# Two-layer vision Mamba on one core: scan outputs by pairs of blocks, a later LayerNorm product, and one turning copy per half unit

## The chip, the cores and the metric

The kernel runs on one core of one Trainium2 chip. Its time is the device time of one launch, in microseconds (us). Three runs of the kernel before took 16030.84, 16043.01 and 16072.04 us; their median, 16043.01 us, is the time before. The profile is one more execution, described below.

## The reference, cut to what matters

Eight images of 64 x 64 positions with 192 channels go through two layers, all in fp32. Layer 0 is a Mamba-2 block with an MLP behind it. Layer 1, the one that the change is in, works on halves of 96 channels:

```
fused = concat(conv_branch(x[..., :96]), ss2d(x[..., 96:])) + x
xr_n = LN(xr) * ln_g + ln_b                   # over 96 channels
xi, z = split(xr_n @ in_proj)                 # 192 + 192
u = silu(depthwise3x3(xi))                    # and u with rows and columns exchanged
y = selective scan of u in four directions    # state 16, 192 channels, 4096 steps
y = y0 + flip(y2) + turned back(y1 + flip(y3)) + D * u
out = (LN(y) * out_norm_g + out_norm_b) * silu(z) @ out_proj    # LN over 192, out 96
```

## The kernel before

**The main loop** is `selective_scan`. It cuts the scan of layer 1 into 3072 units, 384 per image: eight (direction pair, quarter) steps of three channel tiles of 16 units. A unit is 128 rows (8 channels x 16 states) by 1024 positions. For each unit q the loop sends out, engine by engine: a load of the decay input, 512 KB, six units ahead (`fetch`, L1435, on SP's queue); Exp on ScalarE (`decay`, L1440), in pairs, two and three units ahead, after every odd unit; two matmuls that spread the input over the states (`spread`, L1448), one unit ahead, into one of two PSUM buffers; the product with B on VectorE (`weigh`, L1465); the scan on VectorE (`scan`, L1472), the product with C on GpSimd (L1475); and for every four units a sum over states on TensorE with a ScalarE copy (`gather`, L1486 and L1491). `prepare` makes the next tile's inputs, and its transfers `dud` and `dus` are on SP's queue too. Every engine works through its instructions in the order in which they are sent out, and so does SP with the transfers.

**The other work** is written as generators that yield a cost for TensorE work, or None. `Beside` deals it out: each unit has two half units, and in each one `half` (L1280) adds the rate to a credit and runs the current generator until the credit is spent, or until a None, which ends the half unit whatever the credit. A yield of None is therefore a delay: what comes after it is sent out at least one half unit later. Unspent credit is carried, up to one rate. `spread_over` sets the rate when an image begins: 450 / halves + work / (halves - 9 x generators), where `work` is the sum of the known costs. While image i is scanned, these generators run in turn for images i+1 and i-1: `conv0`, `ssd`, `mlp0` (layer 0 of i+1), `conv_branch` and `scan_outputs` (of i-1, with `scan_sums` beside the branch), `scan_inputs` and `transposed` (of i+1). Image 0's scan has no i-1, image 7's has only two `conv_branch` and one `scan_outputs`; layer 0 and the scan inputs of image 0 run ahead of the loop; `scan_sums` and `scan_outputs` of image 7 run behind it, in the tail.

At unit 360 of an image's 384, `Beside.finish` (L1296) runs whatever is left of the generators at once, without regard to yields, since at units 360 to 362 the next image's scan input is loaded (`load`, L1349), and from unit 363 on TensorE projects it (`project`, L1362). At unit 362 the next `conv0` begins.

**`scan_outputs`** (L1193) takes the 4096 positions in eight blocks of 512. Its 192 channels are a tile of 128 rows and one of 64. Per block: load of both; mean by two matmuls (L985), subtraction on VectorE (L989), squares on ScalarE (L992); variance by two matmuls (L1001), Ln and Exp in PSUM on ScalarE (L1003, L1004), product on VectorE (L1008); scale and shift on ScalarE (L1230), two matmuls for z and two Silu (L1234, L1236); product on GpSimd (L1243); projection by two matmuls (L1248, L1249), addition on VectorE (L1253), store. `center` and `normalize`, which hold L985 to L1008, also serve `scan_inputs`, there for 96 channels. PSUM tiles for all of this come from `cx.one` (L88), a ring of four buffers in the loop, shared with `gather`, `project` and `prepare`.

**`transposed`** (L1094) makes u with rows and columns exchanged: four loads of the first 128 channels, each followed by a None (the last by two), then eight copies of 1024 columns on ScalarE (L1114), four for 128 channels and four for 64, through four buffers `part`; each copy is stored by SP (L1122).

Of the kernel before, what the change touches and what calls it, by code (L numbers as in the profile page):

```python
# [105 lines left out]
def setup(cx, cp, dp, tp, p0, p1):  # L106
# [3 lines left out]
    def const(src, shape, tag):  # L110
        t = cp.tile(shape, F32, tag=tag, name=tag)
        nc.sync.dma_start(out=t, in_=src)
        return t

    ident = k["ident"] = cp.tile([128, 128], F32, tag="ident", name="ident")
    make_identity(nc, ident)

# [63 lines left out]
    k["conv3_b"] = const(p1["conv3_b"].unsqueeze(1), [CH, 1], "conv3_b")  # L181
    k["in_proj"] = const(p1["in_proj"], [128, 2 * DI], "in_proj")
    k["out_a"] = const(p1["out_proj"][0:128], [128, CH], "out_a")
    k["out_b"] = const(p1["out_proj"][128:DI], [DI - 128, CH], "out_b")
    k["xp"] = const(p1["xp"].rearrange("g t p m -> p g t m"), [128, 2, 3, NXP], "xp")

    k["dtw"] = cp.tile([NXP, 2, 3, 128], F32, tag="dtw", name="dtw")
# [17 lines left out]
    for n, rows in (("a", slice(0, 128)), ("b", slice(128, DI))):  # L205
        size = rows.stop - rows.start
        for v in ("out_norm_g", "out_norm_b"):
            k[v + n] = const(p1[v][rows].unsqueeze(1), [size, 1], v + n)
    k["dwb"] = cp.tile([128, 3], F32, tag="dwb", name="dwb")
    for i in range(2):  # L210
        nc.sync.dma_start(out=k["dwb"][64 * i : 64 * (i + 1)], in_=p1["dw_b"].rearrange("(j p) -> p j", p=64))
# [22 lines left out]
    for n, c0, c1 in (("xa", 0, 128), ("xb", 128, DI), ("za", DI, DI + 128), ("zb", DI + 128, 2 * DI)):  # L234
        ps = cx.one("ps_b")
        nc.tensor.matmul(ps[: c1 - c0, 0:1], lhsT=k["in_proj"][:CH, c0:c1], rhs=ln_b, start=True, stop=True)
        k["bias_" + n] = cp.tile([128, 1], F32, tag="bias_" + n, name="bias_" + n)
        nc.vector.tensor_copy(k["bias_" + n][: c1 - c0], ps[: c1 - c0, 0:1])
    nc.vector.tensor_scalar_mul(k["in_proj"][:CH], k["in_proj"][:CH], ln_g)
    for n, size in (("m96", CH), ("m192", DI)):  # L240
        k[n] = cp.tile([128, 128], F32, tag=n, name=n)
# [59 lines left out]
def in_turn(items, *stages):  # L301

    for turn in range(len(items) + len(stages) - 1):
        for lag in reversed(range(len(stages))):
            if 0 <= turn - lag < len(items):
                yield from stages[lag](items[turn - lag])
# [669 lines left out]
def center(cx, xs, sizes, means, squares):  # L976

    nc, pin = cx.nc, cx.pin
    n = max(sizes)
    ps = cx.one("ps_mean")
    for i, (x, m) in enumerate(zip(xs, means)):
        pin(nc.tensor.matmul(ps[:n], lhsT=m, rhs=x, start=i == 0, stop=i == len(xs) - 1))  # L985
    yield 1.2 * len(xs)
    yield None
    for x, size in zip(xs, sizes):
        pin(nc.vector.tensor_sub(x[:size], x[:size], ps[:size]))  # L989
    yield None  # L990
    for x, size, s in zip(xs, sizes, squares):
        pin(nc.scalar.activation(s[:size], x[:size], AF.Square))  # L992


def normalize(cx, xs, sizes, means, squares):

    nc, pin = cx.nc, cx.pin
    n = max(sizes)
    ps = cx.one("ps_var")
    for i, (x, m) in enumerate(zip(squares, means)):  # L1000
        pin(nc.tensor.matmul(ps[:n], lhsT=m, rhs=x, start=i == 0, stop=i == len(xs) - 1))  # L1001

    pin(nc.scalar.activation(ps[:n], ps[:n], AF.Ln, bias=cx.k["eps"][:n]))  # L1003
    pin(nc.scalar.activation(ps[:n], ps[:n], AF.Exp, scale=-0.5))  # L1004
    yield 1.2 * len(xs)
    yield None
    for x, size in zip(xs, sizes):
        pin(nc.vector.tensor_mul(x[:size], x[:size], ps[:size]))  # L1008

# [84 lines left out]
def transposed(cx, u):  # L1094

    nc, pin = cx.nc, cx.pin
    with cx.pool("t1") as tp:
        wholes = []
        for n, src in enumerate((u[0], u[2][0:64])):
            wholes.append(tp.tile([src.shape[0], L], F32, tag=f"whole{n}", name=f"whole{n}"))  # L1100

        def load(n, q):
            here = slice(q * L // 4, (q + 1) * L // 4)
            pin(nc.sync.dma_start(out=wholes[n][:, here], in_=(u[0], u[2][0:64])[n][:, here]))

        for q in range(4):
            load(0, q)
            yield from pause(1 if q < 3 else 2)
        front = []
        for whole, dst in zip(wholes, (u[1], u[2][64:128])):  # L1110
            for q in range(4):
                w0 = q * WW // 4
                part = tp.tile([whole.shape[0], L // 4], F32, tag="part", name="part", bufs=4)
                pin(nc.scalar.copy(part.rearrange("p (w h) -> p w h", h=HH), wh(whole)[:, w0 : w0 + WW // 4, :]))  # L1114
                front.append((dst[:, q * L // 4 : (q + 1) * L // 4], part))
                if whole is wholes[0]:
                    load(1, q)
                if q % 2 == 1:
                    yield 1.0
                    yield None  # L1120
                if len(front) == 2:
                    pin(nc.sync.dma_start(out=front[0][0], in_=front.pop(0)[1]))  # L1122
        pin(nc.sync.dma_start(out=front[0][0], in_=front.pop(0)[1]))
# [69 lines left out]
def scan_outputs(cx, y, xn, short, out):  # L1193

    nc, pin, k = cx.nc, cx.pin, cx.k
    parts = (("a", 0, 128), ("b", 128, DI))
    with cx.pool("e1", 2) as ep:
        st = {}
        sizes = (128, DI - 128)
        xns = [ep.tile([128, 512], F32, tag=f"xn{i}", name=f"xn{i}", bufs=1) for i in range(3)]  # L1200
        for v in xns:
            pin(nc.gpsimd.memset(v[CH:], 0.0))

        def cols(r):
            return slice(r * 512, (r + 1) * 512)

        means = [k["m192"], k["m192"][: DI - 128]]

        def load(r):
            st[r] = {}  # L1210
            for n, src in (("a", y[0]), ("b", y[2][0:64])):
                v = st[r][n] = ep.tile([src.shape[0], 512], F32, tag="v" + n, name="v" + n, bufs=7)
                pin(nc.sync.dma_start(out=v, in_=src[:, cols(r)]))
            if r == 0:
                yield from pause(4)
            yield 0.0

        def mean(r):
            pin(nc.sync.dma_start(out=xns[r % 3][:CH], in_=xn[:, cols(r)]))
            sq = st[r]["sq"] = [ep.tile([n, 512], F32, tag=f"sq{n}", name=f"sq{n}") for n in sizes]  # L1220
            yield from center(cx, [st[r]["a"], st[r]["b"]], sizes, means, sq)

        def norm(r):
            yield from normalize(cx, [st[r]["a"], st[r]["b"]], sizes, means, st[r].pop("sq"))

        def gate(r):
            x = xns[r % 3]
            for n in "ab":
                v = st[r][n]
                pin(nc.scalar.activation(v, v, AF.Identity, scale=k["out_norm_g" + n], bias=k["out_norm_b" + n]))  # L1230
            for n, c0, c1 in parts:
                size = c1 - c0
                ps = cx.one("ps_z")[:size]
                pin(nc.tensor.matmul(ps, lhsT=k["in_proj"][:, DI + c0 : DI + c1], rhs=x, start=True, stop=True))  # L1234
                z = st[r]["z" + n] = ep.tile([size, 512], F32, tag="z" + n, name="z" + n)
                pin(nc.scalar.activation(z, ps, AF.Silu, bias=k["bias_z" + n][:size]))  # L1236
                yield 1.2
            sh = st[r]["sh"] = ep.tile([CH, 512], F32, tag="sh", name="sh", bufs=3)
            pin(nc.sync.dma_start(out=sh, in_=short[:, cols(r)]))

        def apply(r):
            for n in "ab":
                pin(nc.gpsimd.tensor_mul(st[r][n], st[r][n], st[r].pop("z" + n)))  # L1243
            yield 0.0

        def project(r):
            ps = cx.one("ps_o")[:CH]
            pin(nc.tensor.matmul(ps, lhsT=k["out_a"], rhs=st[r]["a"], start=True, stop=False))  # L1248
            pin(nc.tensor.matmul(ps, lhsT=k["out_b"], rhs=st[r]["b"], start=False, stop=True))  # L1249
            yield 2.4  # L1250
            yield None
            o = st[r]["o"] = ep.tile([CH, 512], F32, tag="o", name="o")
            pin(nc.vector.tensor_add(o, ps, st[r]["sh"]))  # L1253

        def store(r):
            pin(nc.sync.dma_start(out=out[:, cols(r)], in_=st.pop(r)["o"]))
            yield 0.0

        def ahead(r):
            yield 0.0  # L1260

        yield from in_turn(range(NB), load, ahead, mean, norm, gate, apply, project, store)


class Beside:
# [304 lines left out]
def vision_mamba_pair_kernel(ctx: ExitStack, tc: tile.TileContext, x: bass.AP, p0: dict, p1: dict, out: bass.AP):  # L1570
# [44 lines left out]
    with tc.tile_pool(name="ps_a", bufs=4, space=PSUM) as more:  # L1615
        cx.singles.append(more)
        stages(0)
        beside.finish()
        beside.costs.update(conv_branch=190.0, scan_outputs=78.0)
        cx.singles.remove(more)  # L1620

    def tail():
# [104 lines left out]
```

## Time and profile before

The profiled execution took 16027.31 us, of which its span, first instruction to last, is 16025.4 us. All the times below are microseconds from the span's start.

| stretch | what runs | us |
|---|---|---|
| 0 to 893.9 | ahead of the loop: layer 0 and scan inputs of image 0 | 893.9 |
| 893.9 to 2681.3 | units of image 0 | 1787.4 |
| 2681.3 to 14263.7 | units of images 1 to 6 | 1905.2 to 1941.3 each |
| 14263.7 to 15787.3 | units of image 7 | 1523.6 |
| 15787.3 to 16025.4 | tail | 238.1 |

A group of instructions is shown as line, engine, operation, tiles, shapes, count, then busy us, mean ns of one, and the engine's idle time before them with what ended it. A window is shown as its length and each engine's busy us, the share of full speed that TensorE's clock was granted (PEclk), the share of DMA time in use, and GB/s. A wait is shown as the engine and line that waited, what it waited for, us in total, times, and the longest.

### The profile page before, as it was taken

To read this page: it belongs to the slowest core of one execution; us is meant where nothing else is said; L and a number is where in the kernel's file an instruction comes from. 1 tells how busy PE (TensorE), PEld (TensorE's weight loads), DVE (VectorE), ACT (ScalarE), POOL (GpSimd) and SP (SyncE) were. 2 spreads that over 40 slices of the span, in tenths; PEclk is the share of its full clock that TensorE was granted. 3 is DMA by queue.
4 is the path that set the end of the run, shared out by engine and by line. 5 is a ranking of instruction groups with operands and counts; after the bars stand their busy time and mean duration, and the time that the engine had idled before them with its cause. 6 is when DMAs were issued, how large, how long until landed. Compare 5 with 4: busy or idle time off the path is not lost. (4 is left out here: it accounts for less than half of the span.)

```text
span 16025.4 us, 207140 instructions
## 1 busy us (share of the span) xinstructions
PE 12969.3 (81%) x69608; PEld 4558.8 (28%) x69608; DVE 12232.0 (76%) x9262; ACT 9059.2 (57%) x13776; POOL 10981.2 (69%) x8165
## 2 busy tenths in 40 slices
PE   8977888789887898778878788787888778877766
PEld 4423322333223322233213332233322333211111
DVE  2268887887778877788678886788867887778994
ACT  3355566555665557655466565664656555655653
POOL 3258776876668766687667876678766776667783
PEclk9987888789887898878978799887988879879887
DMA  3288888878787887978878788887888878888885
GB/s 89 86 213 197 212 206 222 198 206 225 199 227 186 214 221 194 226 187 220 218 199 212 191 221 220 209 213 193 220 208 214 205 197 232 202 228 218 212 217 136
DMA packets 1604247, 3243.11 MB, mean 202 GB/s; under 512 B 389424, under 2 KB 843056, under 8 KB 1603184
## 3 DMA queue, kind: packets, MB, share of 16 engines
q1 hardware_dynamic: 1603184, 3229.84, 79.5%
q8 instruction: 556, 9.11, 0.3%
q14 instruction: 507, 4.15, 0.1%
HBM read 2550.93 MB, written 678.18 MB: 201 GB/s over the span
## 5 line engine op out<-in xcount | busy, mean ns | idle before, releaser
L1475 POOL TENSOR_TENSOR h<-h,bc 128x1024 f32<-128x1024 f32 x3072 | 7239.2, 2357 | 1334.9 <-DVE h L1472 1039.1
L1472 DVE TENSOR_TENSOR_SCAN h<-dA,carry,dB 128x1024 f32<-128x1024 f32 x3072 | 7200.3, 2344 | 479.5 <-ACT dA L1440 152.3
L1465 DVE TENSOR_TENSOR dB<-dB,bc 128x1024 f32<-128x1024 f32 x3072 | 3736.6, 1216 | 1665.2 <-PE dB L1448 1625.0
L1440 ACT ACTIVATE dA<-dA,neg_a 128x1024 f32<-128x1024 f32 x3072 | 3373.9, 1150 | 84.9 <-DMA dA<-dld 78.6
L1486 PE MATMUL acc<-h,gather 128*32 128x512 f32 x12288 | 2169.0, 703 | 319.0 <-POOL h L1475 134.7
L1474 POOL COPY carry<-h 128x1 f32<-128x1 f32 x2304 | 421.6, 183 | 2482.3 <-DVE h L1472 2344.5
L1448 PE MATMUL dB<-dus,spread 48*128 48x512 bf16 x6144 | 1401.2, 433 | 886.1 <-DVE h L1472 842.8
L1491 ACT COPY y<-acc 128x512 f32<-128x512 f32 x1536 | 890.2, 580 | 1842.1 <-issue 1014.9
L884 PE MATMUL ps_c<-p,conv_w 128*96 128x512 f32 x2304 | 1165.5, 628 | 37.3 <-ACT p L904 37.3
L1448 PEld LDWEIGHTS <-spread 48*128 48x128 bf16 x6144 | 321.2, 95 | 2969.5 <-issue 1374.7
L687 PE MATMUL ps_y<-X,M 64*64 64x64 f32 x12288 | 622.2, 277 | 433.3 <-issue 200.1
L336 PE MATMUL ps_cv<-pad,diag 64*64 64x512 f32 x6912 | 852.6, 606 | 19.6 <-ACT y L1491 13.0
L615 ACT ACTIVATE M<-ps_d,ln_dt 128x64 f32<-128x64 f32 x3072 | 666.5, 337 | 275.5 <-PE ps_d L621 206.8
L687 PEld LDWEIGHTS ps_y<-X,M 64*64 64x64 f32 x12288 | 567.7, 186 | 602.2 <-issue 256.5
L1486 PEld LDWEIGHTS acc<-h,gather 128*32 128x32 f32 x12288 | 290.7, 115 | 1223.3 <-issue 522.6
L609 ACT COPY bc<-ps_t 64x256 f32<-64x256 f32 x256 | 93.5, 365 | 917.1 <-PE ps_t L604 917.0
L620 PE MATMUL ps_d<-R,after 128*128 128x384 f32 x1024 | 572.7, 650 | 35.5 <-ACT bc L609 16.1
L1440 ACT ACT_TABLE_LOAD x445 | 570.9, 1283 | 7.9
L884 PEld LDWEIGHTS ps_c<-p,conv_w 128*96 128x96 f32 x2304 | 346.2, 167 | 721.9 <-issue 645.2
L1362 PE MATMUL ps_xp<-u,xp 128*128 128x512 f32 x768 | 471.1, 700 | 92.7 <-DMA u<-u 78.5
L1400 POOL TENSOR_TENSOR du<-dl,u 128x1024 f32<-128x1024 f32 x192 | 452.2, 2355 | 96.2 <-DMA bcd<-rows 81.0
L366 PE MATMUL ps_h<-oa,w1a 128*128 128x256 f32 x1536 | 456.0, 417 | 64.0 <-ACT y L1491 23.3
(248 smaller groups left out, 17979.2 us busy)
## 6 DMA issues: line engine op xcount, KB each, us to landing
dA<-dld SPq DMA_DIRECT2D x3072, 512.0 KB
dud<-terms SPq DMA_DIRECT2D x192, 768.0 KB
dus<-dud SPq DMA_DIRECT2D x1152, 128.0 KB
bc<-bcd SPq DMA_DIRECT2D x256, 512.0 KB
y<-yrows SPq DMA_DIRECT2D x256, 384.0 KB
u<-u SPq DMA_DIRECT2D x192, 512.0 KB
dld<-dl SPq DMA_DIRECT2D x192, 512.0 KB
y<-y SPq DMA_DIRECT2D x3072, 32.0 KB
```

The costliest lines, as they stand in the source:

```text
L336: pin(nc.tensor.matmul(ps[64 * b : 64 * (b + 1)].rearrange("p (h w) -> p h w", w=WW), lhsT=diag[:, t, :], rhs=pad[64 * i : 64 * (i + 1), b ...
L615: pin(nc.scalar.activation(M[:, d, h, :], ps[:, h * S : (h + 1) * S], AF.Exp, bias=bias))
L620: pin(nc.tensor.matmul(ps, lhsT=k["after"], rhs=flat(R[:, d * NH : (d + 1) * NH, :]), start=True, stop=False))
L687: pin(nc.tensor.matmul(psy[d][here, h * HP : (h + 1) * HP], lhsT=M[here, d, h, :], rhs=X[here, d, h, :], start=True, stop=True,))
L884: pin(nc.tensor.matmul(ps.rearrange("p (h w) -> p h w", w=WW), lhsT=w[:, t, :], rhs=pad[:, dy : dy + RB, dx : dx + WW], start=t == 0, stop ...
L1440: pin(nc.scalar.activation(dAs[q], dAs[q], AF.Exp, scale=k["neg_a"][:, steps[m][1], t, i : i + 1]))
L1448: pin(nc.tensor.matmul(dBs[q][:, half, :], lhsT=k["spread"][here, i % 2, :], rhs=du_of[n][here, i // 2, :], start=True, stop=True,))
L1465: pin(nc.vector.tensor_mul(dBs[q], dBs[q], of(q)[0]))
L1472: pin(nc.vector.tensor_tensor_scan(order(h, g), order(dA, g), order(dB, g), carry, ALU.mult, ALU.add))
L1475: pin(nc.gpsimd.tensor_mul(h, h, C_))
L1486: pin(nc.tensor.matmul(ps[32 * v : 32 * (v + 1)], lhsT=k["gather"], rhs=hs[q - 3 + v][:, here], start=True, stop=True))
L1491: pin(nc.scalar.copy(y[:, here], ps))
```

## The change

- `scan_outputs` takes four pairs of blocks. The 128 channels of a pair lie beside each other in a tile of 128 x 1024, the 64 channels of both blocks below each other in one of 128 x 512. The helper `both` sends out the two full matmuls and then two 64-row matmuls on different halves of the array. Constants for the 64 channels are held twice (three more small loads in `setup`, and a copy of `bias_zb` on SP's queue).
- The variance product is sent out a half unit later: one more `yield None` in `normalize`, and two ahead of the product in the new `norm`.
- `transposed` yields after each copy, where it did after every second.
- The planner's known cost of `scan_outputs` goes from 78 to 60.

```diff
@@ normalize
     yield 1.2 * len(xs)
     yield None
+    yield None
     for x, size in zip(xs, sizes):
         pin(nc.vector.tensor_mul(x[:size], x[:size], ps[:size]))
@@ transposed
-                if q % 2 == 1:
-                    yield 1.0
-                    yield None
+                yield 1.0
+                yield None
@@ scan_outputs
+        def both(pss, wa, xa, wb, xb):
+            for ps, x in zip(pss, xa):
+                pin(nc.tensor.matmul(ps, lhsT=wa, rhs=x, start=True, stop=False))
+                yield 1.2
+            for ps, low in zip(pss, lows):
+                pin(nc.tensor.matmul(ps, lhsT=wb[low], rhs=xb[low], start=False, stop=True))
+        def parts(p, pss):
+            a, b = st[p]["a"], st[p]["b"]
+            for j, low in enumerate(lows):
+                yield a[:, j, :], pss[j]
+                yield b[low], pss[j][low]
+        def mean(p):
+            pss = [cx.one("ps_mean") for j in range(2)]
+            a, b = st[p]["a"], st[p]["b"]
+            yield from both(pss, k["m192"], [a[:, j, :] for j in range(2)], k["m192"], b)
+            yield 1.2
+            yield None
+            for i, (v, ps) in enumerate(parts(p, pss)):
+                pin(nc.vector.tensor_sub(v, v, ps))
+                if i == 1:
+                    yield None
+            yield None
+            sqs = [ep.tile([128, n, 512], F32, tag=f"sq{n}", name=f"sq{n}", bufs=1) for n in (2, 1)]
+            pin(nc.scalar.activation(wide(sqs[0]), wide(a), AF.Square))
+            pin(nc.scalar.activation(sqs[1][:, 0, :], b, AF.Square))
+            st[p]["sq"] = sqs
+            yield None
+        def norm(p):
+            pss = [cx.one("ps_var") for j in range(2)]
+            sa, sb = st[p].pop("sq")
+            yield from both(pss, k["m192"], [sa[:, j, :] for j in range(2)], k["m192"], sb[:, 0, :])
+            for ps in pss:
+                pin(nc.scalar.activation(ps, ps, AF.Ln, bias=k["eps"]))
+            for ps in pss:
+                pin(nc.scalar.activation(ps, ps, AF.Exp, scale=-0.5))
+            pin(nc.sync.dma_start(out=wide(xns[p % 2])[:CH], in_=xn[:, cols(p)]))
+            yield 1.2
+            yield None
+            yield None
+            for v, ps in parts(p, pss):
+                pin(nc.vector.tensor_mul(v, v, ps))
+            yield None
+        def gate(p):
+            x = xns[p % 2]
+            for n in "ab":
+                v = wide(st[p]["a"]) if n == "a" else st[p]["b"]
+                pin(nc.scalar.activation(v, v, AF.Identity, scale=k["out_norm_g" + n], bias=k["out_norm_b" + n]))
...
+            for j in range(2):
+                ps = cx.one("ps_z")
+                pin(nc.tensor.matmul(ps, lhsT=k["in_proj"][:, DI : DI + 128], rhs=x[:, j, :], start=True, stop=True))
+                pin(nc.scalar.activation(za[:, j, :], ps, AF.Silu, bias=k["bias_za"]))
+                yield 1.2
+            ps = cx.one("ps_z")
+            for j, low in enumerate(lows):
+                pin(nc.tensor.matmul(ps[low], lhsT=k["in_proj"][:, DI + 128 :], rhs=x[:, j, :], start=True, stop=True))
+            pin(nc.scalar.activation(zb, ps, AF.Silu, bias=k["bias_zb"]))
+            yield 1.2
...
-        yield from in_turn(range(NB), load, ahead, mean, norm, gate, apply, project, store)
+        yield from in_turn(range(NP), load, ahead, mean, norm, gate, apply, project, store)
@@ vision_mamba_pair_kernel
-        beside.costs.update(conv_branch=190.0, scan_outputs=78.0)
+        beside.costs.update(conv_branch=190.0, scan_outputs=60.0)
```

More of the change, by code (lines that the diff above doesn't have):

```diff
@@ L113, in const, with twofold @@
         return t
+    def twofold(src, width, tag):
+        t = cp.tile([128, width], F32, tag=tag, name=tag)
+        for i in range(2):
+            nc.sync.dma_start(out=t[64 * i : 64 * (i + 1)], in_=src)
+        return t
     ident = k["ident"] = cp.tile([128, 128], F32, tag="ident", name="ident")
@@ L183, in setup @@
     k["out_a"] = const(p1["out_proj"][0:128], [128, CH], "out_a")
-    k["out_b"] = const(p1["out_proj"][128:DI], [DI - 128, CH], "out_b")
+    k["out_b"] = twofold(p1["out_proj"][128:DI], CH, "out_b")
     k["xp"] = const(p1["xp"].rearrange("g t p m -> p g t m"), [128, 2, 3, NXP], "xp")
@@ L207, in setup @@
         for v in ("out_norm_g", "out_norm_b"):
-            k[v + n] = const(p1[v][rows].unsqueeze(1), [size, 1], v + n)
+            src = p1[v][rows].unsqueeze(1)
+            k[v + n] = const(src, [size, 1], v + n) if n == "a" else twofold(src, 1, v + n)
     k["dwb"] = cp.tile([128, 3], F32, tag="dwb", name="dwb")
@@ L238, in setup @@
         nc.vector.tensor_copy(k["bias_" + n][: c1 - c0], ps[: c1 - c0, 0:1])
+        if n == "zb":
+            nc.sync.dma_start(out=k["bias_zb"][64:128], in_=k["bias_zb"][0:64])
     nc.vector.tensor_scalar_mul(k["in_proj"][:CH], k["in_proj"][:CH], ln_g)
@@ L1195, in scan_outputs, with cols, wide, load @@
     nc, pin, k = cx.nc, cx.pin, cx.k
-    parts = (("a", 0, 128), ("b", 128, DI))
+    NP = NB // 2
+    lows = [slice(64 * j, 64 * (j + 1)) for j in range(2)]
     with cx.pool("e1", 2) as ep:
         st = {}
-        sizes = (128, DI - 128)
-        xns = [ep.tile([128, 512], F32, tag=f"xn{i}", name=f"xn{i}", bufs=1) for i in range(3)]
+        xns = [ep.tile([128, 2, 512], F32, tag=f"xn{i}", name=f"xn{i}", bufs=1) for i in range(2)]
         for v in xns:
             pin(nc.gpsimd.memset(v[CH:], 0.0))
[L1204 to L1214, printed above, removed]
+        def cols(p):
+            return slice(p * 1024, (p + 1) * 1024)
+        def wide(t):
+            return t.rearrange("p j l -> p (j l)")
+        def both(pss, wa, xa, wb, xb):
[4 more added lines that the diff above has]
+                pin(nc.tensor.matmul(ps, lhsT=wb[low], rhs=xb[low], start=False, stop=True))
+        def load(p):
+            a = ep.tile([128, 2, 512], F32, tag="va", name="va", bufs=4)
+            pin(nc.sync.dma_start(out=wide(a), in_=y[0][:, cols(p)]))
+            b = ep.tile([128, 512], F32, tag="vb", name="vb", bufs=4)
+            for j, low in enumerate(lows):
+                pin(nc.sync.dma_start(out=b[low], in_=y[2][0:64, (2 * p + j) * 512 : (2 * p + j + 1) * 512]))
+            st[p] = {"a": a, "b": b}
+            if p == 0:
@@ L1215, in load @@
                 yield from pause(4)
             yield 0.0
[L1218 to L1227, printed above, removed]
+        def parts(p, pss):
[3 more added lines that the diff above has]
+                yield b[low], pss[j][low]
@@ L1228, in gate @@
+        def gate(p):
+            x = xns[p % 2]
             for n in "ab":
-                v = st[r][n]
+                v = wide(st[p]["a"]) if n == "a" else st[p]["b"]
                 pin(nc.scalar.activation(v, v, AF.Identity, scale=k["out_norm_g" + n], bias=k["out_norm_b" + n]))
[L1231 to L1236, printed above, removed]
-                yield 1.2
@@ L1238, in gate @@
-            sh = st[r]["sh"] = ep.tile([CH, 512], F32, tag="sh", name="sh", bufs=3)
-            pin(nc.sync.dma_start(out=sh, in_=short[:, cols(r)]))
-        def apply(r):
-            for n in "ab":
-                pin(nc.gpsimd.tensor_mul(st[r][n], st[r][n], st[r].pop("z" + n)))
-            yield 0.0
[L1246 to L1253, printed above, removed]
@@ L1255, in store @@
-        def store(r):
-            pin(nc.sync.dma_start(out=out[:, cols(r)], in_=st.pop(r)["o"]))
+            za = st[p]["za"] = ep.tile([128, 2, 512], F32, tag="za", name="za")
+            zb = st[p]["zb"] = ep.tile([128, 512], F32, tag="zb", name="zb")
+            for j in range(2):
+                ps = cx.one("ps_z")
+                pin(nc.tensor.matmul(ps, lhsT=k["in_proj"][:, DI : DI + 128], rhs=x[:, j, :], start=True, stop=True))
+                pin(nc.scalar.activation(za[:, j, :], ps, AF.Silu, bias=k["bias_za"]))
+                yield 1.2
@@ new lines, in gate, with apply @@
+            ps = cx.one("ps_z")
+            for j, low in enumerate(lows):
+                pin(nc.tensor.matmul(ps[low], lhsT=k["in_proj"][:, DI + 128 :], rhs=x[:, j, :], start=True, stop=True))
+            pin(nc.scalar.activation(zb, ps, AF.Silu, bias=k["bias_zb"]))
+            yield 1.2
+            sh = st[p]["sh"] = ep.tile([CH, 2, 512], F32, tag="sh", name="sh")
+            pin(nc.sync.dma_start(out=wide(sh), in_=short[:, cols(p)]))
+        def apply(p):
+            for n in "ab":
+                pin(nc.gpsimd.tensor_mul(st[p][n], st[p][n], st[p].pop("z" + n)))
+                yield 0.0
+            if p == NP - 1:
+                yield from pause(4)
@@ new lines, in project, with store @@
+        def project(p):
+            pss = [cx.one("ps_o")[:CH] for j in range(2)]
+            a, b = st[p]["a"], st[p]["b"]
+            yield from both(pss, k["out_a"], [a[:, j, :] for j in range(2)], k["out_b"], b)
+            yield 1.2
+            yield None
+            o = st[p]["o"] = ep.tile([CH, 2, 512], F32, tag="o", name="o", bufs=1)
+            for j, ps in enumerate(pss):
+                pin(nc.vector.tensor_add(o[:, j, :], ps, st[p]["sh"][:, j, :]))
+        def store(p):
+            pin(nc.sync.dma_start(out=out[:, cols(p)], in_=wide(st.pop(p)["o"])))
+            yield 0.0
@@ L1257, in store, with ahead @@
+        def ahead(p):
             yield 0.0
-        def ahead(r):
-            yield 0.0
-        yield from in_turn(range(NB), load, ahead, mean, norm, gate, apply, project, store)
+        yield from in_turn(range(NP), load, ahead, mean, norm, gate, apply, project, store)
 class Beside:
```

## The prediction

> **What bounds the kernel now.** I read the page's busy shares and groups first, then windows around each generator of one image, then VectorE's waits in those windows, then the timeline of ScalarE where the copies run.
>
> ```profile
> PE 12969.3 (81%) x69608; PEld 4558.8 (28%) x69608; DVE 12232.0 (76%) x9262; ACT 9059.2 (57%) x13776; POOL 10981.2 (69%) x8165
> ...
> L1472 DVE TENSOR_TENSOR_SCAN h<-dA,carry,dB 128x1024 f32<-128x1024 f32 x3072 | 7200.3, 2344 | 479.5 <-ACT dA L1440 152.3
> L1465 DVE TENSOR_TENSOR dB<-dB,bc 128x1024 f32<-128x1024 f32 x3072 | 3736.6, 1216 | 1665.2 <-PE dB L1448 1625.0
> ```
>
> No engine is full. VectorE is the loop's pacemaker: a unit alone costs it 2.34 + 1.22 us, and with a 0.13 us gap the last units start every 3.60 us. 3072 units at 3.60 are 11,060 of the loop's 14,893 us; the rest is VectorE's own side work, which the change leaves as it is (ten products and sums of about 0.67 us per pair of blocks, before and after), and its waits. So I count **VectorE's waits**. Windows in image 3 (conv_branch, scan_outputs, scan_inputs, transposed):
>
> ```profile
> core 0: us, PE busy (x) PEld busy (x) DVE busy (x) ACT busy (x) POOL busy (x), PEclk, DMA share, GB/s
> 7695.00:7990.00 295.00, 274.02 (x772) 74.85 (x771) 193.27 (x110) 121.22 (x153) 180.02 (x148) 0.97 0.88 225
> 7990.00:8138.00 148.00, 119.53 (x287) 27.94 (x290) 112.51 (x92) 119.55 (x142) 100.66 (x79) 0.77 0.72 179
> 8138.00:8338.00 200.00, 175.29 (x768) 42.65 (x762) 152.43 (x99) 136.29 (x161) 121.12 (x90) 0.82 0.77 197
> 8338.00:8379.00 41.00, 10.26 (x47) 1.70 (x46) 25.42 (x15) 29.73 (x26) 23.16 (x11) 0.63 0.87 249
> ```
>
> conv_branch is TensorE's. scan_outputs has three engines near 80%, none full: waits in a circle. VectorE's waits in scan_outputs, then in scan_inputs:
>
> ```profile
> DVE va L1008 <- ACT ps_var L1004: 17.0, 7, 4.8
> DVE va L989 <- DMA y<-y: 4.2, 1, 4.2
> DVE dB L1465 <- PE dB L1448: 3.9, 2, 2.6
> DVE o L1253 <- PE ps_o L1249: 3.1, 2, 2.4
> ```
>
> ```profile
> DVE xt L1008 <- ACT ps_var L1004: 19.6, 7, 4.5
> DVE dB L1465 <- PE dB L1448: 19.6, 9, 4.2
> DVE xt L989 <- PE ps_mean L985: 4.2, 1, 4.2
> ```
>
> In both the LayerNorm product's wait for Ln and Exp is among the largest. The copies of `transposed`, on ScalarE:
>
> ```profile
> 8343.18 0.56 ACT L1491 COPY y<-acc 128x512 f32<-128x512 f32 x1
> 8351.04 7.50 ACT L1114 COPY part<-whole 128x1024 f32<-128x1024 f32 x4 [7.30 <-issue]
> 8362.47 3.73 ACT L1114 COPY part<-whole 64x1024 f32<-64x1024 f32 x2 [3.93 <-DMA whole<-u]
> 8366.10 1.04 ACT L1408 CAST terms<-du 128x1024 bf16<-128x1024 f32 x1
> 8367.05 2.18 ACT L1440 ACTIVATE dA<-dA,neg_a 128x1024 f32<-128x1024 f32 x2
> ```
>
> Six copies and their loads hold the queue for 23 us, and the next decay stands behind them: VectorE waits 14.7 us for dA there, once per image.
>
> **The change part by part.** Against the profiled execution's own 16027.3 us:
>
> *The planner's count.* The costs are constants, so the half units follow by stepping the credit. An image's rate falls from 450/768 + 1140.8/705 = 2.204 to 450/768 + 1126.8/705 = 2.184. Half units per generator, images 1 to 6: conv0 147 to 148, ssd 183 to 187, mlp0 178 to 180, conv_branch 109 to 111, scan_outputs 51 to 49, scan_inputs 81 to 85. `transposed` had nine and six were free behind it; now four are left. Its loads go out, then the flush at unit 360 sends **all eight copies in a row**: in images 1 to 6 "one copy per half unit" does not happen. Only image 0's gets its 13.
>
> *scan_outputs, six images.* ScalarE per pair, before: squares 4 x 0.63, Ln 2 x 0.66, Exp 2 x 0.58, scale 4 x 0.80, Silu 4 x 0.68, six table loads of 1.28: 18.6 us. After: three loads, three Silu, Ln and Exp as they were; Square and Identity of 128 x 1024 from SBUF are not in the trace, so I bound them by the 1.15 of L1440 (same shape) and by twice 0.63 or 0.80; with 1.15 and 1.4 it is 12.3 us. 25 us per image leave an engine at 81%. TensorE: sixteen matmuls per pair become twelve slots, if 64-row pairs run together; L368 on the two halves shows four passes in 1.98 us, so they do. But the four-buffer ring now has two buffers for mean, two for variance, three for z: the second variance matmul takes z's first buffer and waits for its Silu, behind scale (2.2), a load (1.28) and Silu (0.69). The next `spread` is queued behind that matmul, and VectorE waits for it. From the order of instructions, ScalarE reaches that Silu 8.7 us after the subtractions, VectorE needs `spread` after 5.9 to 7.1, and matmul and `spread` take 2: 3 to 5 us in two pairs of four. With the first load 4, the first variance 4 to 5, the drain 3 and some 4 more I get 23 where 33 were (34 in the view, with trifles). **-10 x 6 = -60**; bounds 0 (all comes back through the ring) and -18 each, -108.
>
> The ScalarE saving, by row and rule: a 1.28 us load is followed by its Ln 1.30 us after its start, and twelve fewer per image are 15 us, already within the 25. The Trainium skill, "ScalarE: Activation LUTs", section "What ACT_TABLE_LOAD costs", puts a drain of 1.38 us on top, 2.66 in all; by that the twelve would be 32 us. This trace shows no such drain, so the row stands.
>
> *scan_outputs in image 7*, at a lower rate: **-7** (+5 to -15).
>
> *scan_inputs, seven images.* Of 19 us of waiting for Ln and Exp per image (133 in seven), a half unit more, 1.8 us at least, covers most: one wait is 2.7 on average. TensorE then catches up less: it was busy 175 of 200 us and its own wait behind VectorE was 8. At 90% it needs some 185 for the old work in two more units, where VectorE's least is 164; before, 195 plus two bare units, 202. That is -17; I take -12, as the convolution goes out in bigger bursts (up to 16 matmuls in a half unit, before 14). **-84** (0 to -126).
>
> *The other generators* get 3.5 units more for the same matmuls, in stretches that wait for TensorE: **-2 x 6 = -12** (0 to -24). The shifted order has 60 more table loads elsewhere in the program (55 of them for dA): 77 us of ScalarE at 57%, mostly beside other work: **+14** (0 to +56).
>
> *transposed.* Image 0's copies spread out: 21 us of waiting to 16, **-5** (0 to -12). In the six others, eight copies in place of six stand before a decay, 3.8 us more; the cover is a half unit longer. SP is held too: each store waits for its copy, and behind the stores queue u's loads, six-ahead dA loads, `dud`, `dus` and conv0's first loads. u's last load waits for the last store; the projection at unit 363 waits on TensorE, with `spread` behind it: some 5 us. dA's loads are six units ahead and survive. **+6 x 6 = +36** (0 to +220, as the second rival prices it).
>
> *Tail.* Before, a block is one circle of 11.0 us: 9 of ScalarE, then 1.94 waiting for two products and a subtraction. A pair: 11.7 of ScalarE and 4 of VectorE, 15.7 for 22.0. Three circles save 19; filling and draining by pairs costs some 9 (two more matmuls, one at half clock being 2 us; a 2.36 GpSimd product for 1.26). **-10** (+8 to -20). *Setup:* four more issues at 0.5, **+2** (0 to +5).
>
> The clock, in this trace: passes of 128 x 512 start 0.43 us apart, or 0.85 after an idle stretch; PEclk is 0.97 in conv_branch, 0.77 in scan_outputs. With less for TensorE there the share can fall further; my -10 has no TensorE time in it. The Trainium skill, "TensorE: Matmul & The Clock Gate", section "HAM oscillation", has the array at half clock after idle stretches beyond about 3.4 us; by that rule a quarter fewer slots could be given back whole, which speaks against the pairs. The sum does not need them.
>
> **Sum:** -60 - 7 - 84 - 12 + 14 - 5 + 36 - 10 + 2 = **-126 us**. The profiled execution is 16 us below the median of the runs; I apply the sum to the median: 16043 - 126 = **15,917**.
>
> **The rivals.**
> 1. *The waits return on TensorE.* What VectorE no longer waits for Exp, it waits for `spread`, in both stages. For: dB's wait is already 1625 us, and TensorE is at 88% in scan_inputs. Against: TensorE itself waits for VectorE's scan behind each product. Outputs and inputs give nothing: -126 + 151 = +25, **16,068**.
> 2. *The flush decides: slower.* From the first load of `whole` (8339.8) to unit 368 (8428.4) a chain of loads, copies, stores, u's loads, projection and conv0 takes 89 us, covered by 15 units; now it begins 5.5 units later. If it does not shrink, 20 us per image are laid bare; with two more copies (4), u's last load behind the last store (6) and cold matmuls after it (7) it is 37 x 6 = 222 in place of 36: +60, **16,103**. It decides from (162 + 48) / 6 = 35 us per image. For: DMA at 0.87 in that window, with 249 GB/s. Against: u's loads were not late for lack of data but because SP came to them at unit 360.
> 3. *The circle in scan_outputs opens* and the flush costs nothing: 8 more per image in outputs, 5 in inputs, 6 in the flush: -126 - 48 - 35 - 36 = -245, **15,798**.
>
> That the copies don't spread as the change says is counted already.
>
> **Chances.** Forecast 0.52, rival 1 0.18, rival 2 0.13, rival 3 0.17. A measurement of this kernel can tell about 0.3%, 48 us, from no change: faster 0.70 (forecast, rival 3, less the forecast's weak end), same 0.17, slower 0.13. All bounds together reach 15,738 to 16,337; they don't fall together. Leaving out rival 2's half and rival 3's far side: **15,795 to 16,060**.
>
> **What would show it.** Right: L1008 waiting under 5 us per image in scan_inputs; scan_outputs 49 half units with table loads 14 where 26 were; eight copies in a row, VectorE waiting 13 to 20 us for dA at unit 363, and 5 more for `spread`. Wrong: dB's wait grown by more than L1008's fell (rival 1); over 35 us more between units 357 and 368 (rival 2); ring waits of 5 us in every pair; a tail longer than 238 us.

## The result and the profile after

The changed kernel takes **16,099.56 us** (median of 8 runs, 16,079.48 to 16,117.92) where the kernel before, run beside it, took 16,032.67 (8 runs, 16,017.76 to 16,072.04): ratio 1.0043, 95% interval 1.0033 to 1.0053. It is some 67 us slower. The forecast was 126 us faster, and the time lies above the range.

The profiled execution took 16,085.16 us, its span is 16,083.4. On the page, the busy times and the two VectorE groups of the scan:

```profile
PE 12801.7 (80%) x69608; PEld 4565.5 (28%) x69608; DVE 12229.3 (76%) x9262; ACT 8933.2 (56%) x13578; POOL 10942.1 (68%) x8093
...
L1532 DVE TENSOR_TENSOR_SCAN h<-dA,carry,dB 128x1024 f32<-128x1024 f32 x3072 | 7201.2, 2344 | 547.2 <-ACT dA L1500 229.7
L1525 DVE TENSOR_TENSOR dB<-dB,bc 128x1024 f32<-128x1024 f32 x3072 | 3734.6, 1216 | 1738.0 <-PE dB L1508 1730.1
```

No engine has more to do: TensorE, ScalarE and GpSimd are busy for less time than before and VectorE for as long. The added time is all in waits, and two of VectorE's have grown: for dA (152 to 230 us) and for the product that spreads the input (1625 to 1730).

Windows of image 3 (window's length, busy us of each engine, clock, DMA share, GB/s): mlp0, conv_branch, scan_outputs, scan_inputs, and the stretch from scan_inputs' end to the first transfers of the next conv0:

```profile
core 0: us, PE busy (x) PEld busy (x) DVE busy (x) ACT busy (x) POOL busy (x), PEclk, DMA share, GB/s
7329.00:7751.00 422.00, 354.48 (x1684) 153.71 (x1680) 344.69 (x245) 265.75 (x348) 286.54 (x168) 0.92 0.84 215
7751.00:8057.00 306.00, 279.25 (x777) 77.45 (x778) 195.38 (x112) 128.11 (x160) 181.56 (x149) 0.93 0.86 216
8057.00:8202.00 145.00, 93.24 (x286) 24.88 (x284) 111.72 (x90) 91.20 (x106) 92.83 (x68) 0.78 0.78 197
8202.00:8389.00 187.00, 166.52 (x776) 40.87 (x776) 157.37 (x102) 140.94 (x167) 128.99 (x91) 0.88 0.80 203
8389.00:8437.00 48.00, 11.69 (x30) 2.09 (x30) 23.28 (x13) 26.93 (x21) 18.95 (x10) 0.54 0.82 228
```

The two stages that the change rewrites are shorter: scan_outputs 145 us where 148 were, scan_inputs 187 where 200 were. The first row is the surprise. mlp0, in which not a line was changed, stood like this in the kernel before:

```profile
7290.00:7695.00 405.00, 355.28 (x1681) 153.11 (x1684) 342.07 (x242) 254.63 (x339) 282.23 (x166) 0.93 0.85 222
```

The same TensorE work within 1 us, nearly the same clock (0.93 and 0.92), VectorE's work within 3 us, and 17 us longer. VectorE's largest wait in that window, before and after:

```profile
DVE dB L1465 <- PE dB L1448: 47.9, 34, 10.1
```

```profile
DVE dB L1525 <- PE dB L1508: 62.9, 26, 5.9
```

Fewer waits, and together 15 us more. Counted stage by stage over the whole loop (VectorE's gaps of more than 0.1 us between the units at which the planner starts and ends a generator, summed over all images; "around the copies" is transposed, the free units behind it, and units 360 to 362, with image 7's last units), with the four kernels of the first two groups of experiments that change one thing each:

| VectorE idle, us | before | rate alone (b_rate) | flush alone (b_flush) | later product alone (b_late) | pairs alone (b_pairs) | changed kernel | changed kernel, old rate (a_rate) |
|---|---|---|---|---|---|---|---|
| conv0 | 350 | 363 | 447 | 374 | 330 | 499 | 378 |
| ssd | 668 | 678 | 678 | 677 | 680 | 686 | 690 |
| mlp0 | 431 | 535 | 431 | 444 | 431 | 524 | 433 |
| conv_branch | 720 | 740 | 723 | 729 | 728 | 742 | 721 |
| scan_outputs | 253 | 320 | 243 | 248 | 206 | 221 | 212 |
| scan_inputs | 307 | 272 | 306 | 279 | 296 | 199 | 298 |
| around the copies | 143 | 150 | 69 | 174 | 179 | 75 | 155 |

The changed kernel against before: mlp0 +93, conv0 and the copies together +81, conv_branch and ssd +40, scan_inputs -108, scan_outputs -32. Outside the loop the setup costs 4 us more and the tail 17 less (221.1 us).

### The profile page after: what moved, and what is told of

The parts are those of the page before. It is cut to its first block, busy times and chain, and to the rows that moved or that the text cites. A ratio compares the mean times of both kernels' runs of the same rounds, so it can differ in the third digit from the quotient of the medians.

```text
span 16083.4 us, 206660 instructions
## 1 busy us (share of the span) xinstructions
PE 12801.7 (80%) x69608; PEld 4565.5 (28%) x69608; DVE 12229.3 (76%) x9262; ACT 8933.2 (56%) x13578; POOL 10942.1 (68%) x8093
## 5 line engine op out<-in xcount | busy, mean ns | idle before, releaser
L1546 PE MATMUL acc<-h,gather 128*32 128x512 f32 x12288 | 2115.1, 694 | 406.5 <-POOL h L1535 113.3
L1508 PE MATMUL dB<-dus,spread 48*128 48x512 bf16 x6144 | 1332.2, 428 | 774.8 <-DVE h L1532 720.3
```

The lines of the kernel that those rows point to most:

```text
L1508: pin(nc.tensor.matmul(dBs[q][:, half, :], lhsT=k["spread"][here, i % 2, :], rhs=du_of[n][here, i // 2, :], start=True, stop=True,))
L1546: pin(nc.tensor.matmul(ps[32 * v : 32 * (v + 1)], lhsT=k["gather"], rhs=hs[q - 3 + v][:, here], start=True, stop=True))
```

## The experiments

**First question: the parts, or the planner's rate?** My theory on seeing mlp0: the change lowers the planner's known cost of scan_outputs from 78 to 60 (and raises that of transposed from 4 to 8), so the rate falls from 2.204 to 2.184, and this alone deals mlp0's work out worse and leaves no half units for the copies. The rival: the new code itself costs the time.

```diff
a_rate, the changed kernel:
-        beside.costs.update(conv_branch=190.0, scan_outputs=60.0)
+        beside.costs.update(conv_branch=190.0, scan_outputs=74.0)
b_rate, the kernel before:
-        beside.costs.update(conv_branch=190.0, scan_outputs=78.0)
+        beside.costs.update(conv_branch=190.0, scan_outputs=64.0)
b_late, the kernel before (late=True from scan_inputs only):
     yield 1.2 * len(xs)
     yield None
+    if late:
+        yield None
b_pairs: the changed kernel's scan_outputs and setup; normalize and transposed of before; cost 78
```

> The changed kernel, with the planner's cost of scan_outputs at 74 in place of 60, so that an image's rate is the old 2.204 and conv0, ssd, mlp0 and conv_branch take their old 147, 183, 178 and 109 half units; 11 half units are left for transposed, all but its last copy. Packing theory: the lower rate costs 15 us per image in mlp0 and, through the flush, another 15: VectorE's waits in mlp0 go back from 75 to 60 us per image, no wait of 17 us for dA stands after unit 360, and the time is 16,100 - 160 = 15,940 us (15,900 to 15,980). Rival, the pairs and the added half units themselves cost the time (VectorE's new wait for ps_mean in scan_outputs, more table loads): the rate is of no account and the time stays within 30 us of 16,100.

> The kernel before, with the cost of scan_outputs at 64 in place of 78 and nothing else: the rate falls to the 2.184 of the changed kernel, mlp0 takes 180 half units, transposed still gets its nine, with none free behind it, so there is no flush. Packing theory: mlp0 alone gives 6 x 15 us, ssd and conv_branch some 3 each, so 16,033 + 105 = 16,135 us (16,100 to 16,170), with VectorE's waits in mlp0 at 75 us per image. Rival, the pairs and the added half units cost the time: 16,033 within 30 us. If only the flush counted: 16,033 as well.

> The kernel before, with LayerNorm's product one half unit later in scan_inputs alone (not in scan_outputs), rate as before: 85 half units for scan_inputs in place of 81, transposed still gets its nine, two free. Packing theory: scan_inputs loses 15 us of VectorE's waits in each of seven images, as the changed kernel shows (44 to 30 in image 0, 48 to 29 in image 3), and nothing is given back elsewhere: 16,033 - 105 = 15,930 us (15,900 to 15,970). Rival, a half unit more is given back in other generators: 16,033 within 30.

> The kernel before with scan_outputs by pairs alone: LayerNorm's product in scan_inputs and the copies of transposed as they were, cost of scan_outputs at 78, so the rate is as before; 49 half units for scan_outputs in place of 51. From the changed kernel's trace: VectorE's waits in scan_outputs 36 to 33.5 us in each of six images (-16), -16 in image 7, -17 in the tail, +4 ahead of the loop: 16,033 - 45 = 15,988 us (15,960 to 16,020). My forecast had -75 for the same part. If the pairs were what made the changed kernel slow: 16,060 or more.

| kernel | us (runs) | ratio to before, interval |
|---|---|---|
| b_rate | 16,208.26 (4) | 1.0102, 1.0089 to 1.0116 |
| a_rate | 16,010.80 (12) | 0.9985, 0.9975 to 0.9994 |
| b_pairs | 16,002.78 (8) | 0.9977, 0.9967 to 0.9988 |
| b_late | 16,051.25 (12) | 1.0011, 1.0000 to 1.0022 |
| before, run beside them | 16,037.42 (26) | |

**The rate alone costs 171 us**, more than the 105 that I gave it: mlp0 +104 as expected, scan_outputs +67 and conv_branch +20, which I had not expected, scan_inputs -35. The window of mlp0 in b_rate (image 3) and then VectorE's wait in it are those of the changed kernel:

```profile
7364.00:7784.00 420.00, 351.51 (x1680) 151.53 (x1680) 344.05 (x244) 265.62 (x348) 286.64 (x168) 0.93 0.86 216
```

```profile
DVE dB L1465 <- PE dB L1448: 60.5, 24, 6.7
```

With its rate put back, the changed kernel is 89 us faster than it was and faster than before, though not by the 160 expected: mlp0 gave the 91 it should, conv0 and the copies 41 of some 90, and scan_inputs fell back from 199 to 298 us. b_late says the same from the other side: at the old rate the later product takes 28 us from scan_inputs where 105 were expected, and 55 come back in conv0 and around the copies (the profiled executions of a_rate and b_late were each some 30 us over their medians). So at the old rate the later product is not worth its price. The pairs alone are worth 35 us, 10 less than expected.

**Second question: the flush, and is a lower rate simply worse?** b_flush leaves the rate alone and takes away the half units of transposed; p_71 and p_96 move the rate of the kernel with the pairs; a_room gives the changed kernel room for all its copies.

```diff
b_flush, the kernel before, in transposed:
+        yield from pause(11)
         for q in range(4):
             load(0, q)
p_71, from b_pairs (p_96 the same with 96.0):
-        beside.costs.update(conv_branch=190.0, scan_outputs=78.0)
+        beside.costs.update(conv_branch=190.0, scan_outputs=71.0)
a_room, the changed kernel:
-        beside.costs.update(conv_branch=190.0, scan_outputs=60.0)
+        beside.costs.update(conv_branch=190.0, scan_outputs=92.0)
```

> The kernel before, with eleven half units of pause ahead of transposed and nothing else: rate, half units and order of all other generators as before, but only the four loads fit in front of unit 360, and in images 1 to 6 all eight copies are flushed there, as in the changed kernel. Flush theory, from the changed kernel's trace: VectorE loses the 15 us of waiting for dA ahead of unit 360 and waits 17 us for dA and 10 more for the spread product behind it, as u's loads stand on SP's queue behind the copies' stores: +10 to +15 us per image, 16,037 + 75 = 16,110 us (16,080 to 16,140). My forecast's term for the same step, +6 x 6, without its two more copies: 16,050 to 16,073. Rival, the wait is only moved: 16,037 within 25.

> The kernel with the pairs alone, cost of scan_outputs at 71 in place of 78: rate 2.194, halfway between the 2.204 of before and the 2.184 that made the kernel before 171 us slower. By the planner's steps mlp0 now takes 176 half units, of which 14 send out no matmul (13 at 2.204, 23 of 180 at 2.184). Packing theory (a rate is good or bad as it falls in with a generator's own grain): VectorE's waits in mlp0 are 55 to 63 us per image and the time is 16,003 us within 30. Rival, the time falls smoothly with the rate: mlp0 at 67 us, 16,003 + 85 = 16,088 us.

> The kernel with the pairs alone, cost of scan_outputs at 96 in place of 78: rate 2.229; mlp0 175 half units, 14 without a matmul, 17 half units free behind the copies (7 at 2.204). Packing theory: no rule for the sign beyond what the half units show, so within 40 us of 16,003. Rival, the time falls smoothly with the rate, 171 us for 0.020: 16,003 - 210 = 15,790 us.

> The changed kernel whole, with the cost of scan_outputs at 92 in place of 60: rate 2.229, mlp0 175 half units, transposed has all its 13 half units and six are free behind it, so its copies are spread as the change says in every image. Packing and flush theory: of the changed kernel's time, 90 us in mlp0 and 60 to 80 at the flush go; scan_inputs keeps its 29 us of waits or goes back to the 45 of the rate 2.204: 15,940 to 16,020 us, middle 15,970. Rival, one copy per half unit holds VectorE up as often as two: the waits for dA around the copies stay above 15 us per image and the time is 16,020 or more.

| kernel | us (runs) | ratio to before, interval |
|---|---|---|
| b_flush | 16,056.83 (11) | 1.0009, 0.9999 to 1.0018 |
| p_71 | 16,068.84 (9) | 1.0022, 1.0012 to 1.0032 |
| p_96 | 16,263.24 (4) | 1.0144, 1.0130 to 1.0158 |
| a_room | 16,155.37 (5) | 1.0078, 1.0066 to 1.0091 |
| before, run beside them | 16,039.76 (19) | |

The flush alone costs about 17 us, barely told from nothing: 97 us come into conv0, and 74 go around the copies. That is far below the 75 expected from the changed kernel's trace, and inside the forecast's own term for this step (16,050 to 16,073). The packing theory missed the other three as well. p_71 has 79 us of waits per image in mlp0, not 55 to 63, although only 14 of its half units are without a matmul: that count explains nothing; its time is nearer to the smooth rival's 16,088. p_96, at a *higher* rate, is 260 us slower than b_pairs, where the smooth rival had it 210 faster. And a_room, with every copy in its own half unit and six to spare, is slower than the changed kernel, whose copies are flushed. So rates on both sides of 2.204 are worse.

p_96 and a_room have the same rate, 2.229, and differ by the later product and by one copy per half unit (which by p_copies, below, is worth nothing at the old rate). a_room is 108 us faster. VectorE's two largest waits in image 3's scan_inputs are these, in p_96 (8249 to 8452 us) and then in a_room (8201 to 8400 us):

```profile
DVE xt L1017 <- ACT ps_var L1013: 26.2, 8, 7.4
DVE dB L1525 <- PE dB L1508: 15.0, 9, 4.1
```

```profile
DVE dB L1525 <- PE dB L1508: 13.5, 9, 3.5
DVE xt L1018 <- ACT ps_var L1013: 8.1, 6, 2.2
```

Here the wait for Ln and Exp fell by 18 us and did not come back as a wait for the spread product. So what the later product is worth depends on the deal, that is, on which half units the helper work falls into: nothing at 2.204 (a_rate is 8 us slower than p_copies), some 100 us at 2.229.

**Third question: the value of the rate, or the unit at which a generator starts?** In all five kernels with about 60 us of waits in mlp0 it starts at unit 143.0 of the image; at 145.5 or 140.5 in the others. Costs 85 and 92 move the rate but, by the planner's steps, keep 143.0; b_start5 keeps the rate and moves the start.

```diff
p_92, p_85: b_pairs with scan_outputs=92.0 and 85.0
b_start5, the kernel before, ahead of conv0's first line:
+    yield from pause(5)
p_copies: the changed kernel without the None added to normalize, cost 74
```

> The pairs alone, cost of scan_outputs at 92: rate 2.224, nearly the 2.229 that cost the same kernel 260 us at 96. But here conv0 and ssd take 330 half units together, as at 2.204, so mlp0 starts at the same unit as in the kernel before (143.0 of the image; 140.5 at cost 96, 145.5 in the changed kernel and at costs 64 and 71). Phase theory (what counts is at which unit of the scan's own rhythm a generator starts: spread, decay, sums over states and the next tile's inputs recur every 1, 2, 4 and 16 units): VectorE's waits in mlp0 are near 60 us per image, and the time is within 60 us of 16,003. Rate theory (2.204 itself is the good value): waits of 70 us or more, and the time is above 16,150.

> The pairs alone, cost of scan_outputs at 85: rate 2.214; conv0 and ssd again take 330 half units together, mlp0 178, and all later generators start at the same units as with cost 78. Phase theory: VectorE's waits in mlp0 near 60 us per image, time 16,003 within 40 us. Rate theory: halfway to cost 96, 70 us and 16,100.

> The kernel before, with five half units of pause ahead of conv0 and nothing else: rate 2.204 and all work as before, but conv0 and ssd take 335 half units together in place of 330, so mlp0 starts at unit 145.5 of the image, as in the changed kernel; later generators start 1 unit later than before. Phase theory: VectorE's waits in mlp0 are 70 to 80 us per image, and the time is 16,035 + 80 to 120. Rate theory: mlp0 stays at 60, and the time is 16,035 within 30.

> The changed kernel without its third part (LayerNorm's product in scan_inputs is at its old place), and with the cost of scan_outputs at 74, which holds the rate at 2.204: pairs and one copy per half unit, the copies with all their 13 half units, three free behind them. Against the pairs alone (16,003 us): VectorE's wait for dA at the copies falls from 22 to some 14 us in each of six images, 15,955 us (15,930 to 15,990). If one copy per half unit is worth nothing: 16,003 within 20.

| kernel | us (runs) | ratio to before, interval |
|---|---|---|
| p_92 | 16,222.33 (4) | 1.0111, 1.0096 to 1.0126 |
| p_85 | 16,091.66 (5) | 1.0035, 1.0021 to 1.0048 |
| b_start5 | 16,201.23 (4) | 1.0100, 1.0085 to 1.0115 |
| p_copies | 16,002.93 (8) | 0.9981, 0.9971 to 0.9992 |
| before, run beside them | 16,037.83 (12) | |

Each theory meets runs that it cannot explain. p_85 and p_92 came out as the rate theory said (waits of 70 and 85 us, 16,092 and 16,222 us), although mlp0 starts at its old unit. b_start5 came out against it: at the rate of before it is 163 us slower, with the waits of 74 us that the phase theory gave and a time above its range. Nor does the pause only shift the start: by the planner's steps the credit stands differently behind it, so that ssd takes 185 half units for 183 and mlp0 175 for 178. mlp0 in all of them (idle: VectorE, mean of images 1 to 6; the last two columns: TensorE's busy time for the 1104 matmuls that mlp0 itself sends out, and its granted clock from the first to the last of them, means of the same images, counted in the traces):

| kernel | rate | mlp0 starts | half units | idle us | own matmuls us | clock |
|---|---|---|---|---|---|---|
| before | 2.204 | 143.0 | 178 | 61 | 259 | 0.95 |
| b_pairs, p_copies, a_rate, b_late | 2.204 | 143.0 | 178 | 59 to 63 | 257 to 260 | 0.94 to 0.96 |
| p_85 | 2.214 | 143.0 | 178 | 70 | 261 | 0.94 |
| p_92 | 2.224 | 143.0 | 177 | 85 | 265 | 0.92 |
| b_start5 | 2.204 | 145.5 | 175 | 74 | 265 | 0.93 |
| p_71 | 2.194 | 145.5 | 176 | 79 | 265 | 0.93 |
| b_rate, changed kernel | 2.184 | 145.5 | 180 | 76 to 78 | 262 to 263 | 0.93 |
| p_96, a_room | 2.229 | 140.5 | 175 | 72 to 73 | 262 | 0.91 to 0.92 |

mlp0 is not the whole of it: VectorE's idle time in ssd, 668 us before, is 759 in b_start5.

The same matmuls take TensorE 259 us before and 261 to 265 in the kernels with longer waits, and the clock is lower there, 0.94 to 0.91. With the scan's own matmuls, TensorE is busy 11 us longer in p_92 (346 to 357), where VectorE waits 24 us longer. So the clock can account for a part of it, and by these sums not for the whole; whether it lengthens the waits or falls because of them, no run here tells. While VectorE waits for the spread product in mlp0, TensorE is busy with other matmuls for 36 of 46 us per image before, and for 50 of 62 in the changed kernel (images 1 to 6). So the wait is mostly for other matmuls in front of the spread product, and TensorE's idle time lies mostly outside these waits. What is shown is that the deal matters: which half units get how many matmuls, beside which of the scan's own. A rule that tells a good deal from a bad one I did not find. That stays open.

p_copies answers a question of the change itself: one copy per half unit, with room, is worth nothing over b_pairs (16,002.93 and 16,002.78). ScalarE's timeline of its copies in image 3:

```profile
8346.48 7.36 ACT L1123 COPY part<-whole 128x1024 f32<-128x1024 f32 x4 [10.14 <-DMA whole<-u]
8353.74 1.04 ACT L1467 CAST terms<-du 128x1024 bf16<-128x1024 f32 x1
8354.69 2.19 ACT L1499 ACTIVATE dA<-dA,neg_a 128x1024 f32<-128x1024 f32 x2
8359.75 5.64 ACT L1123 COPY part<-whole 64x1024 f32<-64x1024 f32 x3 [2.88 <-DMA whole<-u]
```

They are sent out one by one, but the first waits 10.14 us for its load, and then four run in a row, as before; only then does a decay come between. VectorE's one wait for dA there, 20.7 to 23.9 us in images 1 to 6 of b_pairs, becomes two, of 17.6 to 20.4 us together. That is 3 us per image where 8 were expected, and the time does not show it. b_pairs and p_copies are the fastest kernels found, 35 us or 0.2% below before.

## Why the prediction was wrong

**The step that failed** is "The other generators get 3.5 units more for the same matmuls, in stretches that wait for TensorE: -2 x 6 = -12 (0 to -24)". The rate was treated as a count of half units, with a bound on one side only. By b_rate it is worth **+171 us**, more than all the rest together and of the other sign, and by a_rate, which puts the old rate back into the changed kernel, +89 us. In place of a shorter wait for TensorE, VectorE's wait for the spread product grew, in mlp0 of image 3 from 47.9 to 60.5 us by the rate alone. The planner's count itself came out half unit by half unit (mlp0 180, scan_outputs 49, scan_inputs 85, four left for transposed, eight copies in a row). It told how many half units there are, and not what they hold.

**The remaining terms** came out right in sum, which is in part luck. Without that term the forecast has -114. The changed kernel against b_rate, which has its rate and nothing else of it, is 16,100 against 16,208: -108 (by the two ratios to before, 1.0043 and 1.0102, -95). But beside the old rate the same parts give only -27 (a_rate against before). Nor do they add up: alone, the pairs give -35, the later product +14, the flush +17 and the rate +171, 167 together, and the changed kernel has 67. Term by term, as VectorE's waits:

- *scan_outputs, six images, -60*: -85 against b_rate, -17 against before, -31 for the pairs at the old rate. Image 7, -7: -14 to -16. The ScalarE durations assumed for the new shapes were near: Square 1.06 us (1.15 assumed), scale 1.24 (1.4), 1317 table loads in the program where 1355 - 96 + 60 = 1319 were counted. The ring stall of 3 to 5 us did not come as told: the wait for z's Silu appears once in the window, with 2.3 us. What came in its place is the first mean of a pair, VectorE's longest wait in the stage; below it, the loads of that first pair on SP's queue:

```profile
DVE va L1252 <- PE ps_mean L1225: 15.1, 2, 10.3
DVE va L1275 <- ACT ps_var L1269: 8.0, 3, 3.0
DVE dB L1525 <- PE dB L1508: 6.2, 3, 5.0
```

```profile
8065.03 0.34 SPq L1229 DMA_DIRECT2D va<-y  x1
8065.43 1.12 SPq L1232 DMA_DIRECT2D vb<-y  x2
```

VectorE waited from 8064.8 us on, and the matmuls of the mean started at 8069.76, so the forecast's "first load 4" is 10.3 here. Why SP sent the loads out no earlier is not settled.

- *scan_inputs, -84*: -108 against before, -73 against b_rate, but -28 at the old rate. The wait for Ln and Exp fell as told, if not under 5 us; the two lines that answer to 19.6 and 19.6 before, in image 3:

```profile
DVE dB L1525 <- PE dB L1508: 11.5, 7, 4.1
DVE xt L1018 <- ACT ps_var L1013: 10.6, 6, 4.0
```

In a_rate the second is 7.7 and the first 21.7: at the old rate the wait did return on TensorE, which was my first rival, in this stage. At the rate of the change it did so in part: in b_rate, without the later product, the two lines are 3.6 and 28.9, in that order. At 2.229 it did not (p_96 and a_room).

- *the flush, +36*: +17 by b_flush; in the changed kernel +81 over the stretch of conv0 and the copies, of which the rate alone brings some 20 (b_rate). The mechanism is the one told: the copies, then SP's first load of u, in the changed kernel and before:

```profile
8406.27 7.41 ACT L1124 COPY part<-whole 128x1024 f32<-128x1024 f32 x4 [10.31 <-DMA whole<-u]
8415.69 7.36 ACT L1124 COPY part<-whole 64x1024 f32<-64x1024 f32 x4 [2.01 <-DMA whole<-u]
8422.95 0.57 ACT L1551 COPY y<-acc 128x512 f32<-128x512 f32 x1
8423.43 2.19 ACT L1500 ACTIVATE dA<-dA,neg_a 128x1024 f32<-128x1024 f32 x2
```

```profile
8411.89 9.82 SPq L1131 DMA_DIRECT2D u<-part  x5
8423.07 0.45 SPq L1132 DMA_DIRECT2D u<-part  x1
8423.57 0.58 SPq L1409 DMA_DIRECT2D u<-u  x1
```

```profile
8378.30 0.34 SPq L1349 DMA_DIRECT2D u<-u  x1
```

Unit 360 begins at 8396.3 us in the changed kernel and at 8379.1 before, so u's first load goes out 27 us behind that unit's start where it stood 1 us ahead: SP's queue stands behind the stores, and they behind the copies. TensorE waits 27.1 us for u at one go. The second rival saw this, at 37 us per image; the trace shows 81 / 6 = 13.5, with what the rate brings.

- *tail -10*: -17. *Setup +2*: +4. *Table loads +14* elsewhere: the 60 more come with the rate alone (b_rate has 1416 where the kernel before has 1355); their price is not separable here. *transposed in image 0, -5*: 22.7 to 23.7 us of waits, +1.

**The rivals.** Slower was given 0.13, and by a mechanism (the flush) that is not the one. Rival 1's line, dB's wait grown by more than the product's fell, is met in the page's sums (+105), but the growth is in mlp0, where the change has no line. No rival had the rate.

## What to carry to other kernels

Where helper work is dealt out by a credit rate, a change of one generator's cost re-deals all the others. Price the cost constant as an edit of its own, with both signs, by a run or by the widest difference that the profile shows between two deals. Then compare parts at a fixed deal, and at more than one: here the later product was worth nothing at one rate and some 100 us at another. A stage can get longer with equal busy rows (mlp0 of image 3: 405 to 422 us, TensorE busy 355.3 and 354.5), and is then to be read for the order of the work, not only for its amount.

## What the runs showed of the hardware

Two 64-row matmuls on different halves of the array start together. TensorE's timeline of the first mean in image 3's scan_outputs, four passes of 128 rows (two matmuls), then four of 64 rows (two matmuls):

```profile
8069.76 3.75 PE L1222 MATMUL ps_mean<-va,m 128*128 128x512 f32 x4 [9.23 <-POOL h L1535]
8073.44 1.63 PE L1225 MATMUL ps_mean<-vb,m 64*128 64x512 f32 x4
```

In the trace's records the 64-row passes start in twos at 8073.44 and 8074.45, so the second matmul costs next to no time, as the forecast took it. The Trainium skill, "TensorE: Matmul & The Clock Gate", section "Why this matters for your kernels", says that matmuls in distinct row groups run concurrently; this agrees.

The same lines show the clock: behind 9.23 us of idle time the 128-row passes start 0.85 us apart, and in the next mean, with no idle time ahead, 0.43. Idle time directly ahead does not tell it alone: the fourth mean, with none directly ahead of it, has 0.85 too. The passes of 0.85 us are part of the 10.3 us wait shown above. Over the stage the granted clock is 0.78, where it was 0.77 with a third more slots, so the pairs did not give their TensorE time back to the clock, as the rule on idle stretches in the forecast would have allowed.
